# Expert weights fetched in four pieces with two on their way, in place of three pieces one at a time: a mixture-of-experts kernel on one Trainium2 core

## The chip, the cores and the metric

The program runs on one core of a Trainium2 chip. The time is device microseconds of one execution. Before the change three timed executions gave 574.53, 577.78 and 582.67 us, so the median is 577.78 us. A fourth execution was profiled and took 582.94 us; the profile's span, from the first instruction to the last, is 581.1 us of it.

## What is computed

The reference conditions a batch of 4 x 512 tokens of 512 numbers and sends them through a layer with 32 experts, of which each token uses four. Cut to what matters:

```python
h = relu((n * x + sum(x)) * q_emb @ W2 + b2)          # 2048 tokens x 512
t = rmsnorm(h) * norm_w
scores = softmax(t @ gate_w.T); topk_w, topk_ids = top_k(scores, 4)
# each (token, expert) pair gets a row of that expert's buffer of C = 512 rows; later ones are dropped
gu = buf[e] @ w13[e]            # 512 -> 2 x 256
act = silu(g) * u
eo = act @ w2[e]                # 256 -> 512
out = x + h + shared(t) + sum over a token's experts of eo * weight
```

Everything is float32. One expert's weights, w13 and w2 together, are 128 partitions x 3072 numbers, 1536 KB.

## The kernel before, in words

The program has three stages: routing (up to about 122 us), the loop over blocks of expert rows (about 122 to 512 us), and an ending that finishes the shared expert and adds everything up.

**Blocks.** The rows of each expert are cut into units of 64. Two units in the order of the experts make a block, and a block can hold the end of one expert and the start of the next. How many units an expert has depends on the routing; this input gives 121 units, that is 61 blocks. Some experts fill eight units, others one. For a block TensorE turns the rows (`b_transpose`), multiplies them by w13 of the first unit's expert straight out of the ring and by w13 of the second unit's expert out of a copy (`b_up`, line 1151), turns the product (`b_turn`), and multiplies by w2 (`b_down`, line 1174). VectorE and ScalarE make the copies (line 1062). POOL gathers the rows of later blocks (`gather`, line 1094, five blocks ahead) and adds each block's result to two arrays in memory with accumulating indirect DMAs (`scatter`, line 1102, two per block). The results wait in five buffers `eo` for their scatters.

**The order on TensorE.** `body(i)` is written out by hand, two blocks to a pair. At the start of an even body come the turns and transposes, `b_down(i - 2)`, then `may_copy(i)`, then `b_down(i - 1)` and the two `b_up` of block i; the body of i + 1 adds its own `b_up`. `may_copy(i)` makes TensorE wait until the semaphore `ready` has reached the number of experts that the pair needs, and then lets the copies start.

**The ring.** Weights lie in a ring of `NBUF = 8` slots in SBUF, one expert to a slot. The first eight experts are loaded whole (`fetch`, line 458, 1536 KB each) during routing. The 24 others follow in the loop through `refill(e)` (lines 474 to 484): SP waits until TensorE has passed the last block of expert e - 8 (the semaphore `b_PE` against a number that the routing produced, `rel`), then for each of three pieces starts the transfer and waits until it has landed, and at last raises `ready`. SP runs the refills strictly in order of the experts and does nothing else in this stage, so one refill starts only when the previous one has landed whole. Each slot has one semaphore, `wlane`.

The names that the later steps use: line 481 is the launch of a piece together with SP's waits ahead of it, line 483 is SP's raising of `ready`.

Of the kernel before, what the change touches and what calls it, by code (L numbers as in the profile page):

```python
# [207 lines left out]
def adaln_moe_kernel(nc, stack, x, xt, cond, W3, b3, W2, b2, norm_w, gate_w, wx, sg, su, sd, out):  # L208
# [23 lines left out]
    NBUF = 8  # L232
    WROW = HC * 2 * I + IC * H
# [6 lines left out]
    k = Program(nc, stack)  # L240
# [11 lines left out]
    def keep(name, shape, dtype):  # L252
        n = SIZE[dtype]
        for s in shape[1:]:
            n *= s
        t = k.sbuf(name, shape, dtype, top[0])
        top[0] += -(-n // 32) * 32
        return t
# [35 lines left out]
    before = keep("before", [P, P], F16)  # L294
# [40 lines left out]
    ring = k.sbuf("ring", [P, NBUF * WROW], F32, top[0])  # L335
# [68 lines left out]
    k.lane_group("yin", 16)  # L404
    k.lane_group("ost", 4)
    wlane = [k.sem(f"wl{i}") for i in range(NBUF)]
    k.sem("ready")
    k.sem("go", "PE")
    joins = {e: k.sem("j" + e) for e in ENGINES}
# [59 lines left out]
    def announce(e):  # L469
        k.raw("SP", lambda s: (s.wait_ge(k.sems[wlane[e % NBUF]], 16), s.sem_inc(k.sems["ready"], 1)))  # L470

    PIECES = 3

    def refill(e):

        a, n, lane = (e % NBUF) * WROW, WROW // PIECES, k.sems[wlane[e % NBUF]]

        def fn(s):
            s.wait_ge(k.sems["b_PE"], k.reg["rel"][e - NBUF])
            for i in range(PIECES):  # L480
                s.dma_start(out=ring[:, a + i * n : a + (i + 1) * n], in_=wx[e][:, i * n : (i + 1) * n]).then_inc(lane, 16)
                s.wait_ge(lane, 16 + 16 * (PIECES * (e // NBUF - 1) + i + 1))
            s.sem_inc(k.sems["ready"], 1)  # L483
        k.raw("SP", fn)

# [175 lines left out]
    def taken(g):  # L661

        t0, t1 = GROUPS[g]
        n = t1 - t0
        fi, ht, mk = idf[:, t0:t1, :], hot[:], mask[:, t0:t1, :]
        op("DVE", lambda e: e.tensor_copy(fi, ids[:, t0:t1, :K]), r=[ids[:, t0:t1, :]], w=[fi])
        op("DVE", lambda e: e.tensor_tensor(
            ht.rearrange("p t k e -> p (t k) e"),
            fi.rearrange("p t k -> p (t k)").unsqueeze(2).to_broadcast([P, n * K, E]),
            iota_e[:].unsqueeze(1).to_broadcast([P, n * K, E]), ALU.is_equal), r=[fi, iota_e[:]], w=[ht])  # L670

        op("DVE", count(mk, ht.rearrange("p t k e -> p t e k")), r=[ht], w=[mk])

    def totals(g):
        t0, t1 = GROUPS[g]
        mk = mask[:, t0:t1, :]
        if g + 1 < len(GROUPS):
            c0, c1 = cum[:, g, :], cum[:, g + 1, :]
            op("DVE", count(csum[:], mk.rearrange("p t e -> p e t")), r=[mk], w=[csum[:]])
            op("DVE", lambda e: e.tensor_tensor(c1, c0, csum[:], ALU.add), r=[c0, csum[:]], w=[c1])  # L680
        else:

            c0 = cum[:, g, :]
            op("DVE", count(csum[:], mk.rearrange("p t e -> p e t")), r=[mk], w=[csum[:]])
            op("DVE", lambda e: e.tensor_tensor(cumj[:], c0.unsqueeze(2).to_broadcast([P, E, NJ]),
                                                csum[:].unsqueeze(2).to_broadcast([P, E, NJ]), ALU.add),
               r=[c0, csum[:]], w=[cumj[:]])
# [15 lines left out]
    def places(g):  # L703

        t0, t1 = GROUPS[g]
        n = t1 - t0
        pp = GU[0][:, 0 : n * E].rearrange("p (t e) -> p t e", t=n)
        sl, pk = sel[:, 0:n], ppk[:, 0:n, :]
        for i in range(n):
            op("DVE", lambda e, i=i: e.tensor_tensor(sl[:, i], hot[:, i], pp[:, i : i + 1, :].to_broadcast([P, K, E]),  # L710
                                                     ALU.mult),
               r=[hot[:, i], GU[0][:]], w=[sl[:, i]])
        dve_scalar(within[:, t0:t1, :], pp, float(C - 1), None, ALU.is_lt)
        op("DVE", lambda e: e.tensor_reduce(pk.rearrange("p t k -> p (t k)"), sl.rearrange("p t k e -> p (t k) e"),
                                            AX.X, ALU.add), r=[sl], w=[pk])

    def places2(g):
        t0, t1 = GROUPS[g]
        n = t1 - t0
        pk, pc = ppk[:, 0:n, :], ppc[:]  # L720
        b0, b1, b2, b3 = (y[:, 0:n, :] for y in blk)
        l, e1 = lo[g % 2][:, 0:n, :], ej[g % 2][:, 0:n, :]
        dve_scalar(b0, pk, float(P), None, ALU.is_ge)
        dve_scalar(b3, pk, float(C), 4096.0, ALU.is_ge, ALU.mult)
        dve_scalar(pc, pk, float(C - 1), None, ALU.min)
        op("DVE", lambda e: e.scalar_tensor_tensor(b1, pk, float(2 * P), b0, ALU.is_ge, ALU.add), r=[pk, b0], w=[b1])
        op("DVE", lambda e: e.scalar_tensor_tensor(b3, idf[:, t0:t1, :], float(NJ), b3, ALU.mult, ALU.add),
           r=[idf[:, t0:t1, :], b3], w=[b3])
        op("DVE", lambda e: e.scalar_tensor_tensor(b2, pk, float(3 * P), b1, ALU.is_ge, ALU.add), r=[pk, b1], w=[b2])

        op("DVE", lambda e: e.scalar_tensor_tensor(l, b2, float(P), pc, ALU.mult, ALU.subtract), r=[b2, pc], w=[l])
        op("DVE", lambda e: e.tensor_tensor(e1, b2, b3, ALU.add), r=[b2, b3], w=[e1])
# [50 lines left out]
    def one_hots(g, t):  # L783
        place_hots(g, t, t % 2 == 0)
        block_hots(g, t)
# [26 lines left out]
    for t in range(NT):  # L812

        g, i = divmod(t - 5, TB)
        first, rest = [], []
        if g in (0, 1) or g == 2 and i < 2:
            u = GROUPS[g][0] + 2 * (i - 2)
            first, rest = [([lambda: taken(g)], [lambda: totals(g)]),
                           ([lambda: places(g)], [lambda: places2(g)]),
                           ([lambda: one_hots(g, u)], [lambda: one_hots(g, u + 1)]),  # L820
                           ([lambda: one_hots(g, u)], [lambda: one_hots(g, u + 1)])][i]
# [22 lines left out]
        b, i = divmod(t, TB)  # L844
# [285 lines left out]
    for e in range(NBUF, E):  # L1130
        refill(e)
# [304 lines left out]
```

## Time and profile before

| | |
|---|---|
| timed executions | 574.53, 577.78, 582.67 us |
| profiled execution | 582.94 us |
| span of its profile | 581.1 us |
| PE busy | 552.9 us, 95% of the span |
| POOL, DVE, ACT busy | 285.3, 287.2, 221.0 us |
| DMA moved | 120.21 MB, mean 207 GB/s |
| queue of SP's and ACT's own transfers (q1) | 83.24 MB |
| queue of POOL's indirect DMAs (q0) | 34.39 MB |

PE is TensorE, DVE VectorE, ACT ScalarE, POOL GpSimd and SP SyncE; a q behind a name is that engine's sequencer, which waits and issues. "Lnnn" is a line of the kernel. A view of waits lists who waited for whom, with total us, times and the longest. The chain of waits follows the work that ended last back from the end of the program, each step with its start and length in us. The view by stretches gives the busy time of an engine in a stretch of the span, the clock granted to TensorE there (1.00 is full) and the busy share of the DMA engines.

### The profile page before, as it was taken

To read this page: it belongs to the slowest core of one execution; us is meant where nothing else is said; L and a number is where in the kernel's file an instruction comes from. 1 tells how busy PE (TensorE), PEld (TensorE's weight loads), DVE (VectorE), ACT (ScalarE), POOL (GpSimd) and SP (SyncE) were. 2 spreads that over 40 slices of the span, in tenths; PEclk is the share of its full clock that TensorE was granted. 3 is DMA by queue.
4 is the path that set the end of the run, shared out by engine and by line. 5 is a ranking of instruction groups with operands and counts; after the bars stand their busy time and mean duration, and the time that the engine had idled before them with its cause. 6 is when DMAs were issued, how large, how long until landed. Compare 5 with 4: busy or idle time off the path is not lost.

```text
span 581.1 us, 7789 instructions
## 1 busy us (share of the span) xinstructions
PE 552.9 (95%) x2518; PEld 237.7 (41%) x2518; DVE 287.2 (49%) x807; ACT 221.0 (38%) x428; POOL 285.3 (49%) x237
## 2 busy tenths in 40 slices
PE   8999999999999999999999999991999995989997
PEld 5565665443333433344333433330333341334342
DVE  2569998956544554445544555441454443400322
ACT  2548757623533444333433444330244332310100
POOL 1202202245666657666676667672366674422910
PEclk9999999999999999999999999997899997999999
DMA  9786979757677867888888888886778885338931
GB/s 308 259 332 231 319 294 341 257 174 196 131 162 170 200 141 195 216 205 195 211 205 214 214 202 233 200 203 162 201 170 207 205 202 138 59 41 297 390 119 72
DMA packets 45742, 120.21 MB, mean 207 GB/s; under 512 B 8020, under 2 KB 9048, under 8 KB 44600
## 3 DMA queue, kind: packets, MB, share of 16 engines
q1 hardware_dynamic: 29440, 83.24, 43.5%
q0 software_dynamic: 15040, 34.39, 30.5%
q10 hardware_dynamic: 1208, 1.92, 0.9%
q8 instruction: 26, 0.43, 0.3%
q14 instruction: 28, 0.23, 0.1%
HBM read 89.36 MB, written 34.36 MB: 213 GB/s over the span
## 4 chain that ended last, share of the span: by engine, by line
PE 73%; DMA 20%; DVE 3%; ACT 2%; issue 1%; POOL 0%; SPq 0%; DVEq 0%; ACTq 0%
PE GU L1151 27%; DMA ring<-in_L_ffn_w_dram 19%; PE D L1174 15%; PE D L542 7%; PE TX L542 4%; PE GU L542 4%; PE TX L535 3%; PE TA L535 3%; PE D L1313 2%; PE TA L1313 2%; PE TX L874 2%; DMA z<-in_xt_dram 1%; PE TA L542 1%; PE D L592 1%; PE D L552 1%
## 5 line engine op out<-in xcount | busy, mean ns | idle before, releaser
L1102 POOL DMA_INDIRECT y_rows<-eo,sidx x122 | 180.2, 1477 | 115.8 <-ACT eo L1178 52.2
L1151 PE MATMUL GU<-ring,xT 128*64 x488 | 215.3, 594 | 0.6 <-issue 0.6
L1151 PE MATMUL GU<-up,xT 128*64 128x512 f32 x488 | 215.3, 594 | 0.0
L1174 PE MATMUL D<-ring,actT 128*64 x244 | 115.2, 614 | 18.1 <-SPq L483 17.8
L1151 PEld LDWEIGHTS GU<-ring,xT 128*64 128x64 f32 x488 | 67.1, 138 | 141.2 <-issue 141.2
L1174 PE MATMUL D<-down,actT 128*64 128x512 f32 x244 | 115.2, 614 | 0.0
L1159 DVE TENSOR_TENSOR act<-silu,GU 128x256 f32<-128x256 f32 x61 | 25.7, 421 | 176.7 <-ACT silu L1158 176.7
L1094 POOL DMA_INDIRECT rows<-h_rows,idx x66 | 68.8, 1042 | 44.7 <-DVE wrow L1186 14.4
L1158 ACT ACTIVATE silu<-GU 128x256 f32<-128x256 f32 x61 | 23.5, 385 | 148.3 <-PE GU L1151 148.3
L1062 ACT COPY up<-ring 128x1024 f32 x62 | 64.3, 1037 | 22.0 <-PEq L1077 16.2
L1151 PEld LDWEIGHTS GU<-up,xT 128*64 128x64 f32 x488 | 67.2, 138 | 0.0
L1178 ACT ACTIVATE eo<-D,wrow 128x512 f32<-128x512 f32 x61 | 41.9, 688 | 56.7 <-PE D L1174 48.1
L1174 PEld LDWEIGHTS D<-ring,actT 128*64 128x64 f32 x244 | 31.2, 139 | 77.8 <-issue 77.8
L1062 DVE COPY up<-ring 128x1024 f32 x62 | 44.7, 721 | 20.9 <-PEq L1077 20.1
L542 PE MATMUL D<-W_sb,z 128*128 128x512 f32 x120 | 54.3, 595 | 0.6 <-POOL z L557 0.6
L1062 DVE COPY down<-ring 128x1024 f32 x62 | 42.5, 712 | 1.5 <-PE D L1174 1.4
L1090 DVE COPY xT<-TX 128x512 f32<-128x512 f32 x62 | 40.0, 686 | 5.0 <-PE TX L535 2.8
L557 POOL TENSOR_SCALAR z<-z,vs,q_sb 128x512 f32<-128x512 f32 x12 | 9.6, 802 | 56.6 <-ACT junk L548 56.4
L535 PE MATMUL TX<-ident,rows 128*128 128x128 f32 x248 | 32.3, 273 | 0.0
L1165 ACT COPY actT<-TA 128x256 f32<-128x256 f32 x61 | 22.7, 373 | 23.7 <-PE TA L535 22.4
L1174 PEld LDWEIGHTS D<-down,actT 128*64 128x64 f32 x244 | 31.3, 139 | 0.0
L542 PEld LDWEIGHTS D<-W_sb,z 128*128 128x128 f32 x120 | 21.7, 190 | 22.8 <-issue 22.0
(207 smaller groups left out, 559.1 us busy)
## 6 DMA issues: line engine op xcount, KB each, us to landing
ring<-in_L_ffn_w_dram SPq DMA_DIRECT2D x72, 512.0 KB, 4.4
ring<-in_L_ffn_w_dram SPq DMA_DIRECT2D x8, 1536.0 KB, 8.6
y<-y_rows SPq DMA_DIRECT2D x8, 1024.0 KB, 13.0
h_rows<-h SPq DMA_DIRECT2D x16, 256.0 KB, 4.9
y_rows<-hid SPq DMA_DIRECT2D x16, 256.0 KB, 4.2
out_dram<-y SPq DMA_DIRECT2D x16, 256.0 KB, 2.5
z<-in_xt_dram SPq DMA_DIRECT2D x14, 256.0 KB, 5.3
y_rows<-eo,sidx POOLq DMA_INDIRECT x122, 4.4
```

The lines of the kernel that those rows point to most:

```text
L535: last = e.transpose(o, i, ident[:n, :n])
L542: last = e.matmul(o, lhsT=lt, rhs=rh, start=(n == 0), stop=(n == len(terms) - 1))
L1062: return e.copy(dst, src) if eng == "ACT" else e.tensor_copy(dst, src)
L1090: return op("DVE", lambda e: e.tensor_copy(xt[:], pt[:].rearrange("p (c t) -> p c t", c=HC)), r=[pt[:]], w=[xt[:]])
L1094: op("POOL", lambda e: e.indirect_dma_start(out=r[:], out_offset=None, in_=h_dram, in_offset=bass.IndirectOffsetOnAxis(ap=idx[:, i : i + 1 ...
L1102: op("POOL", lambda e, o=o, y=y, at=at: e.indirect_dma_start(out=y, out_offset=bass.IndirectOffsetOnAxis(ap=at, axis=0), in_=o, in_offset= ...
L1151: last = e.matmul(pg[h * U : (h + 1) * U, :], lhsT=xt[:, c, h * U : (h + 1) * U], rhs=w, start=(c == 0), stop=(c == HC - 1))
L1158: op("ACT", lambda e: e.activation(s, pg[:, 0:I], AF.Silu), r=[pg[:]], w=[s])
L1159: op("DVE", lambda e: e.tensor_tensor(a, s, pg[:, I : 2 * I], ALU.mult), r=[s, pg[:]], w=[a])
L1174: last = e.matmul(po[h * U : (h + 1) * U, :], lhsT=at[:, c, h * U : (h + 1) * U], rhs=w2, start=(c == 0), stop=(c == IC - 1))
L1178: op("ACT", lambda e: e.activation(o, po[:], AF.Copy, scale=w), r=[po[:], w], w=[o])
L1313: last = e.matmul(BK[j][:], lhsT=t_act[:, i, j * P : (j + 1) * P], rhs=sd_sb[:, i, :], start=start and i == 0, stop=stop and i == IC - 1)
```

## The change

A slot is refilled in four pieces of 768 numbers a partition (384 KB) in place of three of 1024 (512 KB). SP launches the first two pieces one behind the other. After that it waits for the piece two before the next one, launches the next, and at the end waits for the last two; then it raises `ready` as before. Pieces 0 and 2 count on the slot's semaphore `wlane`, pieces 1 and 3 on a second semaphore of the slot, `wlane2`. The wait for the release of the slot, the order of the refills and the bytes stay. So does every instruction of the other engines: apart from shifted line numbers they run the same lists, and on SP 96 launches stand where 72 stood.

```diff
     wlane = [k.sem(f"wl{i}") for i in range(NBUF)]
+    wlane2 = [k.sem(f"wm{i}") for i in range(NBUF)]
...
-    PIECES = 3
+    PIECES = 4
 
     def refill(e):
 
-        a, n, lane = (e % NBUF) * WROW, WROW // PIECES, k.sems[wlane[e % NBUF]]
+        a, n = (e % NBUF) * WROW, WROW // PIECES
+        lanes = [(k.sems[wlane[e % NBUF]], 16), (k.sems[wlane2[e % NBUF]], 0)]
+        before = 8 * PIECES * (e // NBUF - 1)
 
         def fn(s):
             s.wait_ge(k.sems["b_PE"], k.reg["rel"][e - NBUF])
-            for i in range(PIECES):
-                s.dma_start(out=ring[:, a + i * n : a + (i + 1) * n], in_=wx[e][:, i * n : (i + 1) * n]).then_inc(lane, 16)
-                s.wait_ge(lane, 16 + 16 * (PIECES * (e // NBUF - 1) + i + 1))
+            for i in range(PIECES + 2):
+                lane, first = lanes[i % 2]
+                if i >= 2:
+                    s.wait_ge(lane, first + before + 16 * (i // 2))
+                if i < PIECES:
+                    s.dma_start(out=ring[:, a + i * n : a + (i + 1) * n], in_=wx[e][:, i * n : (i + 1) * n]).then_inc(lane, 16)
             s.sem_inc(k.sems["ready"], 1)
         k.raw("SP", fn)
```

## The prediction

> **What bounds the kernel now.** I read first who TensorE waited for. The page gives PE 95% of the span, and in the loop, which runs from 122 us to about 512 us, its view of waits has one entry that counts:
>
> ```profile
> PE D L1174 <- SPq L483: 17.8, 2, 11.9
> ```
>
> Two times TensorE stood before a `b_down` (line 1174) for SP's `ready` (line 483), 11.9 us and, as the rest of 17.8, 5.9 us. So the weights came too late twice; all other waits of PE in the loop together are under 2 us. Next, the waits of SP's queue between 230 and 487 us:
>
> ```profile
> SPq L481 <- DMA ring<-in_L_ffn_w_dram: 159.2, 38, 5.8
> SPq L483 <- DMA ring<-in_L_ffn_w_dram: 76.8, 19, 5.7
> SPq L481 <- PE D L1174: 1.7, 2, 1.3
> ```
>
> In these 257 us SP waited 236 us for its own pieces to land and 1.7 us for a slot to be released. Here the stream of pieces is the limit, not the ring's size. Before 230 us it was otherwise: there the same view has 37.2 us of waits for TensorE's release. The 19 refills after 230.06 us (a launch at that time follows the last such wait) end with the last landing at 486.8, so one refill takes 256.7 / 19 = 13.5 us. The chain of waits then shows both stalls and what they cost:
>
> ```profile
> 345.57 3.58 PE D L1174 x16
> ...
> 399.13 3.99 DMA ring<-in_L_ffn_w_dram
> ...
> 403.14 3.54 DMA ring<-in_L_ffn_w_dram
> ...
> 407.01 3.68 PE D L1174 x8
> 410.69 7.62 PE GU L1151 x32
> ...
> 419.78 3.58 PE D L1174 x16
> ...
> 482.82 3.98 DMA ring<-in_L_ffn_w_dram
> ...
> 487.12 3.64 PE D L1174 x8
> 490.76 6.87 PE GU L1151 x32
> ...
> 499.09 3.58 PE D L1174 x16
> ```
>
> Without a stall a pair's `b_down` group starts every 11.92 us (333.65, 345.57 and so on in the same chain). From 345.57 on, starts at 393.25 and 405.17 were due; the second came at 419.78, 14.6 us late. From 419.78 five pairs later is 479.38 and six is 491.30; it came at 499.09, 7.8 us late. The two stalls cost 22.4 us together, 4.6 us more than the waiting. The view by stretches shows where the rest is:
>
> ```profile
> core 0: us, PE busy (x), PEclk, DMA share, GB/s
> 357.40:393.20 35.80, 35.80 (x183) 1.00 0.83 207
> 393.20:419.80 26.60, 14.68 (x63) 0.74 0.71 177
> ```
>
> The granted clock fell to a mean of 0.74 around the stall; right after it eight matmuls took 3.68 us where sixteen take 3.58. A stall is paid about 2.3 us more than it waits.
>
> Last, the sizes of the transfers on the ring, median us from launch to landing:
>
> ```profile
> ring<-in_L_ffn_w_dram SPq DMA_DIRECT2D x72, 512.0 KB, 4.4
> ring<-in_L_ffn_w_dram SPq DMA_DIRECT2D x8, 1536.0 KB, 8.6
> ```
>
> Three times the bytes take twice the time: 1024 KB more cost 4.2 us, so 512 KB cost 2.1 us for their bytes and 2.3 us that do not depend on them. The serial refill pays the 2.3 us three times.
>
> **What a refill takes after the change.** From these two rows a piece of 384 KB takes 2.3 + 1.6 = 3.9 us alone. The first pieces of a refill go out 0.33 us apart (the duration of a launch in the rows of line 481). The first lands at 3.9, the second after its own bytes, 1.6 us later, at 5.5. The third is launched at 3.9 and lands at 7.8, the fourth at 5.5 and lands at 9.4. So I take 9.4 us in place of 13.5. The ends: from below 7.0 us, the fastest whole 1536 KB transfer of line 458, one fixed part for all bytes; from above 4 x 3.9 = 15.5 us, if nothing overlaps. I hold to the middle because the trace has an overlap on this very queue: two whole transfers launched at 99.16 and 99.67 us landed at 107.28 and 111.86, 12.7 us for both where one after the other at 8.1 us would be 16.2.
>
> [...]
>
> **What refill time is enough.** Were TensorE never stalled, the refill that ended the first stall (the 13th after 230.06) would be due at 407.01 - 11.92 = 395.1, the last one at 487.12 - 5.9 - 14.6 = 466.6. That allows 165.0 / 13 = 12.7 us and 236.5 / 19 = 12.45 us a refill. 9.4 us is well under both, so both stalls go entirely and SP goes back to waiting for releases. A faster refill then gains nothing more, because TensorE is busy without a gap from 357 to 393 us (35.80 of 35.80).
>
> **The other terms.** Instructions: 24 more launches, each 0.33 us, and as many waits on SP, behind which only the next piece and the next refill are queued; they lie in the refill time. The chain's "SPq L483" step and the gap behind it, 0.1 us a refill, stay. TensorE, VectorE, ScalarE and POOL run the same lists: nothing. Bytes are the same, in rows of 3 KB for 4 KB. What stands beside it is the indirect traffic, which shares the DMA engines: scatters landed in a median of 3.7 us while no piece was on its way (206 to 218 us) and 4.6 us with one on its way (230 to 393 us). With two I take another 0.9, 5.5 us, bounds 4.6 and, with twice the excess added again, 6.4. A scatter to one array waits for the one before it to that array (0.3 us more), so a pair needs 2 x 5.8 = 11.6 us of its 11.92: still hidden, barely. The ending after 512 us has no ring traffic before or after and moves as a whole.
>
> **The sum.** 582.9 - 22.4 = 560.5 us. The median before, 577.8, is 5.2 us below the profiled run; since runs differ in how long they stall, I expect the shorter ones to lose the same stalls, and take 560.5 for the median after, 3.0% below.
>
> **Rivals.**
>
> *The pieces slow each other and the gathers, and some stall stays.* For: in the page's slices the DMA engines are 0.8 busy through the loop. Against: a rate of 207 GB/s there, and 341 in an earlier slice. At 12.9 us a refill the last lands at 230.06 + 19 x 12.9 = 475.2, 8.6 us late, plus about 4 us of low clock: 573 us.
>
> *No overlap: slower.* The queue could work a second transfer only when the first has landed, so that the change does not do what it says. Then a refill takes 15.5 + 0.1 us, the last lands at 230.06 + 19 x 15.6 = 526.5, 39.7 us later than now, and all that follows with it: 623 us. It is late from 12.45 us a refill on, and slower by 2% (6.4 us over 582.9) from (486.8 + 6.4 - 230.06) / 19 = 13.85 us. For: the size rows, with 2.3 us a piece. Against: the two whole transfers above.
>
> *Scatters become the bound.* At 6.4 us a pair needs 2 x 6.7 = 13.4 us on POOL's chain, 1.5 over. Five `eo` buffers are 2.5 pairs, 29.8 us, of which a block's own two scatters take about 8; some 20 us of lag are free. Over the 20 pairs from 230 to 467 us, 30 us of lag leave 10 to pay: 570 us. From 5.66 us (11.92 / 2 - 0.3) lag builds up; it is lost again whenever SP waits for a release. Against: the longest scatter in the serial stream was 6.6 us, the median 4.6.
>
> **Chances.** Forecast 0.75; some stall stays 0.13; scatters 0.06; no overlap 0.06. The forecast's own width is about 3 us (three runs before, without the stalls' differences). The range runs from 557, the forecast less its width, to 573, the price of a remaining stall. "Faster" means below 566 (2% under the median, about what a measurement of this kernel can tell from no change): the forecast and a third of the remaining stalls, 0.80. Same: the rest of those and the scatters, 0.14. Slower: no overlap, 0.06.
>
> **What would show it.** Right: no PE wait for SP's `ready` in the loop; pairs 11.92 us apart throughout; clock 1.00 from 357 to 500; SP's waits for TensorE's release after 230 us well above 1.7; a refill of 8 to 11 us. The step on contention is wrong if scatters land above 5.7 us in the median and ScalarE's `eo` waits for them. The whole is wrong if a refill takes over 12.45 us, or if `b_down` waits for something not named here.

## The result, and the profile after

Four executions of the changed kernel took 560.13, 560.37, 561.19 and 562.46 us, median 560.78 us. The kernel before, with one execution more, has a median of 580.22 us (574.53 to 585.22). The ratio is 0.970, 95% interval 0.961 to 0.979: faster. The profiled execution took 562.46 us, 20.5 us less than the profiled one before. Each ratio further below is against executions of the kernel before taken beside that experiment; their medians were 578.27 to 582.75 us.

In PE's view of waits the entry on SP's `ready` is gone, and the longest left is 2.2 us, in the ending. (Line numbers have moved: 481 is now 488, 483 is 489, 1151 is 1157, 1174 is 1180, 1102 is 1108, 1094 is 1100; 535, the transposes, is 541; 542, the matmuls of the shared expert, is 548. D, GU and TX are the banks that matmuls write.) SP's waits between 230 and 487 us, in us in total, times and longest:

```profile
SPq L489 <- DMA ring<-in_L_ffn_w_dram: 81.3, 19, 5.4
SPq L488 <- DMA ring<-in_L_ffn_w_dram: 69.2, 30, 4.6
SPq L488 <- PE D L1180: 12.7, 5, 6.3
SPq L488 <- PE TX L541: 0.5, 2, 0.3
```

SP waited 150.5 us for pieces, where it was 236, and 12.7 us for TensorE to release a slot, where it was 1.7. The last `ready` came at 436.9 us, not 486.8. From the launch at 229.4 us on that is 207.5 us, 12.7 + 0.5 of them waits for a release, so a refill took 194.3 / 19 = 10.2 us. The stretches that held the first stall are now full:

```profile
core 0: us, PE busy (x), PEclk, DMA share, GB/s
230.00:300.00 70.00, 70.00 (x356) 1.00 0.87 223
300.00:400.00 100.00, 100.00 (x506) 1.00 0.90 242
400.00:450.00 50.00, 50.00 (x254) 1.00 0.83 206
```

TensorE is busy without a gap at the full clock, with the DMA engines 0.83 to 0.90 busy. The chain of waits runs through TensorE alone here, a pair every 11.92 us:

```profile
344.94 3.58 PE D L1180 x16
...
356.85 3.58 PE D L1180 x16
...
368.76 3.58 PE D L1180 x16
```

Over the 29 intervals between the pairs' first `b_down` matmuls the loop lost 0.1 us against a step of 11.91 us; before it lost 22.6. The loop also began 0.6 us earlier (130.43 for 131.02). Behind the loop 2.6 us came back, most of them here, in the chain of the changed kernel:

```profile
489.70 3.63 PE TX L548 x8
493.33 2.21 issue
495.54 5.40 PE GU L548 x8
```

In the chain of the kernel before, the same gap and the same eight matmuls were shorter:

```profile
515.99 1.77 issue
517.76 3.70 PE GU L542 x8
```

A gap a little earlier grew from 0.46 to 0.91 us. The view by stretches shows that the clock fell behind the gap:

```profile
core 0: us, PE busy (x), PEclk, DMA share, GB/s
357.00:489.00 132.00, 131.09 (x648) 1.00 0.76 180
495.50:501.00 5.50, 5.46 (x11) 0.69 0.01 3
```

### The profile page after: what moved, and what is told of

Read it like the earlier page. It is cut to its first block, busy times and chain, and to the rows that moved or that the text cites. A ratio compares the mean times of both kernels' runs of the same rounds, so it can differ in the third digit from the quotient of the medians.

```text
span 560.6 us, 7813 instructions
## 1 busy us (share of the span) xinstructions
PE 549.7 (98%) x2518; PEld 237.1 (42%) x2518; DVE 287.2 (51%) x807; ACT 220.8 (39%) x428; POOL 287.4 (51%) x237
## 4 chain that ended last, share of the span: by engine, by line
PE 92%; DVE 3%; ACT 2%; issue 1%; DMA 1%; POOL 0%; SPq 0%; DVEq 0%; ACTq 0%
PE GU L1157 37%; PE D L1180 20%; PE D L548 7%; PE TX L541 5%; PE TX L548 5%; PE GU L548 4%; PE TA L541 4%; PE D L1319 2%; PE TA L1319 2%; PE TX L880 2%; PE TA L548 1%; DMA z<-in_xt_dram 1%; PE D L598 1%; PE D L558 1%; PE D L1312 1%
## 5 line engine op out<-in xcount | busy, mean ns | idle before, releaser
L1180 PE MATMUL D<-ring,actT 128*64 x244 | 111.3, 599 | 0.2 <-issue 0.2
L1180 PE MATMUL D<-down,actT 128*64 128x512 f32 x244 | 111.3, 599 | 0.0
L1100 POOL DMA_INDIRECT rows<-h_rows,idx x66 | 70.5, 1068 | 33.6 <-issue 13.1
L548 PEld LDWEIGHTS D<-W_sb,z 128*128 128x128 f32 x120 | 21.7, 190 | 22.4 <-issue 22.0
(207 smaller groups left out, 561.2 us busy)
```

The costliest lines, as they stand in the source:

```text
L548: last = e.matmul(o, lhsT=lt, rhs=rh, start=(n == 0), stop=(n == len(terms) - 1))
L1100: op("POOL", lambda e: e.indirect_dma_start(out=r[:], out_offset=None, in_=h_dram, in_offset=bass.IndirectOffsetOnAxis(ap=idx[:, i : i + 1 ...
L1180: last = e.matmul(po[h * U : (h + 1) * U, :], lhsT=at[:, c, h * U : (h + 1) * U], rhs=w2, start=(c == 0), stop=(c == IC - 1))
```

## The experiments

Theory L: only the length of a whole refill counts, against the 12.45 us that TensorE leaves for it. A piece pays about 2.3 us whatever its size (the estimate from the medians before, 4.4 us for 512 KB and 8.6 us for 1536 KB), and two on their way hide part of that. Rival O: two transfers on their way are needed as such. Rival P: the small pieces help. Rival S: larger transfers hold up POOL's scatters.

**Four pieces, one at a time.** The changed piece size without the overlap, on the loop of the kernel before:

```diff
-    PIECES = 3
+    PIECES = 4
```

> Four pieces of 384 KB, one at a time. Theory L (only the length of a whole refill against the 12.45 us that TensorE allows decides; a piece pays 2.3 us fixed and 4.1 us per MB): 4 x 3.9 + 0.1 = 15.6 us a refill, the last lands at about 526 us, 620 to 630 us, slower than the kernel before. Rival P (the smaller pieces or their 3 KB rows are what helps, not the second one on its way): about 560 us.

Measured: 621.85 us (620.67 to 622.27), ratio 1.067 (1.059 to 1.074). Its view of PE's waits, and the row of the pieces (KB each, median us to landing):

```profile
PE D L1174 <- SPq L483: 50.7, 5, 16.6
```

```profile
ring<-in_L_ffn_w_dram SPq DMA_DIRECT2D x96, 384.0 KB, 3.7
```

Five stalls. A refill took 15.4 us and the last landed at 526.2. Rival P falls: alone, the smaller piece costs 39 us. The loop lost 61.3 us for 50.7 of waiting, 2.1 us more a stall, the low clock again: its mean was 0.74 between 380 and 430 us and 0.88 between 430 and 530.

**Two pieces, one at a time.** Nothing overlaps, but one fixed part less:

```diff
-    PIECES = 3
+    PIECES = 2
```

> Two pieces of 768 KB, one at a time, one semaphore. Theory L: 2 x (2.3 + 3.15) + 0.1 = 11.0 us a refill, under 12.45, so no stall and 560 to 563 us with nothing overlapped. Rival O (the overlap of two transfers is what is needed, a serial stream always stalls): stalls stay, 570 to 585 us.

Measured: 562.12 us (560.74 to 564.25), ratio 0.965 (0.958 to 0.973), no wait of PE for SP, a refill of 11.6 us. Rival O falls: one changed digit, without a second semaphore, removes both stalls too.

**Three pieces of 512 KB, two on their way.** In the changed kernel, with the counts of the two semaphores kept right for an odd number of pieces:

```diff
-    PIECES = 4
+    PIECES = 3
...
-        before = 8 * PIECES * (e // NBUF - 1)
+        turn = e // NBUF - 1
...
-                    s.wait_ge(lane, first + before + 16 * (i // 2))
+                    s.wait_ge(lane, first + 16 * (turn * ((PIECES + 1 - i % 2) // 2) + i // 2))
```

> Three pieces of 512 KB as before, but two on their way. Theory L: 8.8 us by the sizes, about 9.6 us as the changed kernel's refill (10.2 where 9.4 was worked out) came out a little longer: no stall, 560 to 562 us, the same as the changed kernel. Rival P: the 512 KB pieces keep their stalls, 570 us and more.

Measured: 563.13 us (559.92 to 564.62), ratio 0.965 (0.957 to 0.974), a refill of 9.6 us, no stall, 1.1 us above the range expected. With two on their way, pieces of 512 KB do as well as pieces of 384 KB, so rival P falls here too.

**Eight and six pieces, two on their way.** `PIECES = 8` and `PIECES = 6` in the changed kernel, nothing else:

> Eight pieces of 192 KB, two on their way. Theory L: a piece takes 2.3 + 0.8 = 3.1 us, four rounds and the last piece's bytes 13.2 us, and with the factor by which the changed kernel's refill came out longer (10.2 / 9.4) 14.3 us a refill, over 12.45: the last lands near 229.4 + 19 x 14.3 = 501 us, 34 us after it is due, and with some low clock the time is 590 to 602 us, slower than the kernel before although two are on their way. Rival O (two on their way is what counts): about 561 us.

> Six pieces of 256 KB, two on their way. Theory L: a piece takes 3.35 us, three rounds and the last bytes 11.1 us, with the same factor 12.0 us a refill, just under 12.45: 560 to 566 us, at most one short stall. A time over 572 us would say that the limit of 12.45 us or the sizes are wrong.

Measured: eight pieces 604.76 us (602.25 to 608.76), ratio 1.045 (1.036 to 1.054), a refill of 14.6 us, the last `ready` at 509.3, where 590 to 602 us, 14.3 and 501 were expected. Six pieces 566.18 us (564.84 to 571.21), ratio 0.980 (0.971 to 0.989), a refill of 12.5 us. PE's waits, of eight pieces and of six:

```profile
PE D L1180 <- SPq L489: 38.4, 4, 13.7
```

```profile
PE D L1180 <- SPq L489: 2.1, 1, 2.1
```

With two on their way throughout, the kernel goes from no stall through one to four as the refill passes 12.5 us. That is the limit read from the profile before, within what these runs resolve. Six pieces came out just above the 560 to 566 us expected, at a refill of 12.5 us where 12.0 was expected. In its profile the stall cost the loop 2.5 us, and the loop also began 4.6 us later than in the changed kernel. A part of that is the clock in the routing: its mean between 50 and 60 us was 0.83 there and 1.00 in the changed kernel, an estimated 1.7 us (0.17 of 10 us). The rest is not explained here.

**The serial kernel without the scatters.** Three pieces one at a time as before, with the scatters left out:

```diff
-        for h in range(2):
+        for h in range(0):
```

> The kernel before, three pieces one at a time, with the scatters (line 1102) left out, so the experts' results are not added up. Theory L with contention as a part of the piece's time: pieces land in 3.6 to 3.8 us in place of 4.4, a refill takes 11.0 to 11.5 us, no stall, 557 to 563 us. If the piece's time is its own and not the scatters', 4.4 us and both stalls stay and the time is 570 us or more.

Measured: 559.30 us (558.62 to 560.50), ratio 0.967 (0.960 to 0.974), no stall. A refill took 11.9 us, longer than the 11.0 to 11.5 expected, and 1.5 us less than with the scatters. So about a tenth of the refill's time before came from the scatters beside it; without them the serial stream is in time. That the gathers, which stay, make up the difference from what was expected was not tested.

**One transfer of 1536 KB.** The fewest fixed parts:

```diff
-    PIECES = 3
+    PIECES = 1
```

> A slot refilled by one transfer of 1536 KB. Theory L: 8.6 to 9.5 us a refill, no stall, 560 to 562 us. Rival S (a long run of ring packets holds up the scatters and gathers until TensorE waits for them): scatters wait longer on POOL than in the changed kernel (34.7 us over 30 waits there) and the time is 565 us or more.

Measured: 582.52 us (577.92 to 589.81), ratio 1.011 (1.003 to 1.019). The refill is the shortest of all, 7.8 us, `ready` is never late, and yet nothing is gained: its executions lie among those of the kernel before (572.74 to 589.86 us). So theory L is wrong where it says that only the refill's length counts. Here rival S holds. PE's longest wait is now another:

```profile
PE TX L535 <- DMA rows<-h_rows,idx: 10.8, 6, 3.2
```

It waits for gathered rows. (This profiled execution, 577.92 us, was the shortest of ten; its loop lost 14.6 us.) POOL's timeline in that stretch (start, us, engine, line, what; in brackets its idle time before) shows why:

```profile
379.65 1.40 POOL L1102 DMA_INDIRECT y_rows<-eo,sidx  x1 [0.30 <-issue]
381.36 1.00 POOL L1094 DMA_INDIRECT rows<-h_rows,idx  x1 [0.30 <-issue]
385.15 1.42 POOL L1102 DMA_INDIRECT y_rows<-eo,sidx  x1 [2.79 <-DMA y_rows<-eo,sidx]
386.87 1.40 POOL L1102 DMA_INDIRECT y_rows<-eo,sidx  x1 [0.30 <-issue]
388.57 1.26 POOL L1094 DMA_INDIRECT rows<-h_rows,idx  x1 [0.30 <-DVE wrow L1187]
393.91 1.42 POOL L1102 DMA_INDIRECT y_rows<-eo,sidx  x1 [4.07 <-DMA y_rows<-eo,sidx]
```

A block's first scatter starts 8.8 us after the one before (385.15, 393.91), where TensorE makes a block every 5.96 us; POOL stands 2.8 and 4.1 us until an earlier scatter has landed, and the gathers stand behind it in the same queue.

**The same without the scatters.** Both edits together:

> The single transfer of 1536 KB a slot, with the scatters left out, so the experts' results are not added up. If TensorE's late gathers in the single-transfer kernel come from POOL standing behind scatters that wait for one another, they are on time here and the time is 557 to 561 us, as with the scatters left out of the kernel before (559.3). If the gathers' own transfers are what the large transfer holds up, PE still waits some 10 us for gathered rows and the time is 570 us or more.

Measured: 560.35 us (two executions, 560.22 and 560.48), ratio 0.962 (0.951 to 0.973), no PE wait for gathers. The edit takes the scatters' bytes away too, but a gather did not land sooner for it. From issue to landing it took, with the scatters and without them:

```profile
DMA to landing us min/median/max: 3.3/4.3/9.3
DMA to landing us min/median/max: 3.3/4.8/8.5
```

So it is POOL's order behind the scatters that made the gathers late, not the gathers' own transfers. (The first line has 55 of the 66 gathers.)

**Bytes on their way, or the length of a row.** A row of the single transfer is 12 KB, one of the changed kernel 3 KB. Two kernels with the whole 1536 KB on their way in shorter rows: the four pieces launched at once, each on its own semaphore,

```diff
-        lanes = [(k.sems[wlane[e % NBUF]], 16), (k.sems[wlane2[e % NBUF]], 0)]
-        before = 8 * PIECES * (e // NBUF - 1)
+        lanes = [(k.sems[wlane[e % NBUF]], 16)] + [(k.sems[w[e % NBUF]], 0) for w in wlane2]
+        before = 16 * (e // NBUF - 1)
...
-            for i in range(PIECES + 2):
-                lane, first = lanes[i % 2]
-                if i >= 2:
-                    s.wait_ge(lane, first + before + 16 * (i // 2))
+            for i in range(PIECES + 4):
+                lane, first = lanes[i % 4]
+                if i >= 4:
+                    s.wait_ge(lane, first + before + 16)
```

and the changed kernel with `PIECES = 2`, so both on their way:

> The four pieces of the changed kernel with all four launched at once, each on a semaphore of its own: 1536 KB on their way as in the single transfer, but in rows of 3 KB as in the changed kernel. Theory A (the bytes on their way at once hold up the scatters): refills of 8 to 9 us, POOL's scatters wait as in the single transfer (60.6 us over 20 waits there against 34.7 in the changed kernel), gathers come late and the time is 575 to 590 us. Theory R (the length of a row decides, since scatter packets wait behind single long ring packets of 12 KB): waits as in the changed kernel and 560 to 562 us.

> Two pieces of 768 KB, both on their way: 1536 KB at once in rows of 6 KB. Theory A: 575 to 590 us, as with four pieces at once. Theory R: between the changed kernel and the single transfer, 563 to 575 us, above four pieces at once.

Measured: four at once 573.47 us (570.77 to 574.86), ratio 0.987 (0.982 to 0.992); two at once 578.14 us (574.71 to 583.63), ratio 0.995 (0.991 to 0.999): both less than 2% from the kernel before. The wait for gathers is back, of four at once:

```profile
PE TX L541 <- DMA rows<-h_rows,idx: 8.5, 7, 1.8
```

Theory R alone falls, since 3 KB rows did not save it; theory A gives the cause but not the whole size, as four at once is a little under its range, and with rows of 3, 6 and 12 KB the time rises from 573 to 578 to 583. At rows of 3 KB, 768 KB on their way took 560.8 us and 1536 KB took 573.5, so the bytes on their way are the larger part. The row's length may add to it, but it was not taken alone: the number of transfers and the refill's length change with it.

All in one table. "Refill" is the mean of the 19 from about 230 us on, from the first launch to `ready`; "lag" is how long after ScalarE wrote an even block's result its first scatter started on POOL (mean, and the longest over all blocks), both from the starts and ends in the traces. One profiled execution stands behind each row's refill, wait and lag.

| kernel | refill us | PE's wait for `ready` | lag us, mean (longest) | median us |
|---|---|---|---|---|
| four, one at a time | 15.4 | 50.7 | 0.3 (5.5) | 621.9 |
| eight, two on their way | 14.6 | 38.4 | 0.3 (4.9) | 604.8 |
| three, one at a time (before) | 13.5 | 17.8 | 0.4 (5.8) | 580.2 |
| six, two | 12.5 | 2.1 | 0.3 (5.8) | 566.2 |
| two, one at a time | 11.6 | 0 | 3.0 (12.9) | 562.1 |
| four, two (changed) | 10.2 | 0 | 0.8 (7.0) | 560.8 |
| three, two | 9.6 | 0 | 5.6 (19.7) | 563.1 |
| four at once | 8.7 | 0 | 9.9 (28.6) | 573.5 |
| two at once | 8.1 | 0 | 9.8 (31.3) | 578.1 |
| one transfer | 7.8 | 0 | 10.0 (30.0) | 582.5 |

## Why the prediction was right

**The bound** was right: the two stalls were the stream's, and went with a shorter refill whichever way it was shortened (two pieces one at a time, three pieces with two on their way, scatters left out).

**The limit of 12.45 us** was right: of the kernels that were run, the one at 12.5 stalled once, all under 12 did not wait for `ready`, all from 13.5 up stalled two to five times.

**The refill** was worked out as 9.4 us and measured 10.2. The term that was small is the piece with another beside it: 2.3 us and 1.6 us are from rows where one transfer was on its way. Alone, a piece of 384 KB took 3.7 us where 3.9 was worked out; with another on its way the median of a 512 KB piece was 5.0 us, against 4.4 alone. It did not matter with 2 us to spare.

**The clock** after a stall, 2.3 us a stall: about right, 2.1 us a stall with five stalls and 45.4 - 38.4 = 7.0 us over four, 1.8 a stall.

**The sum** said 22.4 us less than the profiled run, and it was 20.5. The loop gave 22.5 and its earlier start 0.6. The 2.6 us that came back are the ending, which did not move as a whole: two gaps were together 0.9 us longer, and the clock fell behind the second, 1.7 us more for the eight matmuls. So the sign of a clock of 1.00 from 357 to 500 us held through the loop, to 489 us, and not behind it. In the three executions without a profile the granted clock was 1.00, and they took 560.1 to 561.2 us.

**The median** at 560.5 came out at 560.78, and that it came so close is in part luck: it took the 22.4 us off one profiled execution, and rested on the view that executions before differ in how long they stall. With 13 executions of the kernel before beside the serial kernels, they spread from 572.7 to 589.9 us; those of the changed kernel lie within 2.3 us. The mean granted clock of the shortest was 0.991, of the longest 0.983, so the longest had more time at a low clock; that the stalls make all of this spread was not shown.

**No overlap**, the slower rival, did not occur, but its price was right: 623 us was worked out, and the kernel without overlap took 621.85. Of SP's pieces, one at a time and beside other traffic, those of 384 KB took 3.7 us in the median and those of 512 KB 4.4 us, so three quarters of the bytes took 0.84 of the time.

**Scatters as the bound** was priced at 20 us of free lag. In the changed kernel the longest lag was 7.0 us, so it stayed hidden; at 19.7 (three pieces, two on their way) still no wait, at 28.6 and above TensorE waited. So the mechanism is real, with the point from which it decides between 19.7 and 28.6 us. Its place was named too narrowly: TensorE is reached through the gathers that queue behind the scatters. ScalarE did wait for scatters before it wrote `eo`, 11.5 us with the single transfer and 6.0 us in the changed kernel, as much as before; but TensorE's views of waits show none for that. The scatters' time to landing, taken as 5.5 us, is not in the changed kernel's page. The landing records of its trace, of which some are missing, give a median of 4.8 to 5.1 us between 230 and 393 us, depending on how many records are asked of a scatter: above the 4.6 before, under what was taken, and under the 5.66 us from which lag was to build up. The same count gives 6.0 us for the single transfer and 6.3 for four at once, above it. Three pieces, two on their way, have 5.3 to 5.4 us and yet a lag of up to 19.7, so lag can build up for a while below that median too. The lag itself went from 0.4 to 0.8 us.

One transfer of 1536 KB gives the shortest refill here, 7.8 us, and at 582.5 us the slowest kernel of those that do not wait for `ready`: the measurement decides against it in this kernel.

## What to carry to other kernels

When a stream of transfers makes the compute engine wait, work out from the chain how long one item may take, and change the stream only until it is below that with a little to spare; here everything between 9.6 and 11.6 us gave the same time within 0.5%. Here fewer pieces (two, one at a time, 562.1 us) and a second transfer on its way (four pieces, 560.8 us) did it equally. Beyond that, more bytes on their way can be paid by the other transfers beside them, here the chain of accumulating scatters and all that queues behind it (573.5 to 582.5 us with 1536 KB on their way), so read that queue's lag before making transfers larger.

## What the runs showed of the hardware

The granted clock fell after a gap of 2.21 us in the ending of the changed kernel, but not after every such gap. The gap in the ending is 1.5 to 2.4 us in these profiles. Eight matmuls behind it took 5.40 us after 2.21 us (changed kernel) and 5.40 after 2.09 (three pieces, two on their way), but 3.70 after 2.14 (two pieces, one at a time) and 3.70 after 2.37 (four at once). In the changed kernel the granted clock was 0.69 on the mean there (495.5 to 501 us): its trace has it at 0.50 for 3.4 us, from 496.9 to 500.3. At the two stalls of the kernel before it stood at 0.50 for 13.7 and for 6.8 us. Gaps of 2.09 and 2.21 us had the slow matmuls behind them and gaps of 2.14 and 2.37 us had not, so the length of a gap alone does not tell whether it costs 1.7 us more.
